# Graph attention inside a four-layer network: scores with keys on partitions, no maximum, and sums over keys on TensorE

## The chip, the cores and the metric

The kernel runs on one core of one Trainium2 chip. The metric is the device time of one execution in microseconds (us). The kernel before takes 2527.05 us, the median of 3 runs (2525.28 to 2527.08). A core has five engines that matter here, each with its own queue: TensorE (PE in the profile, with its weight loads as PEld), VectorE (DVE), ScalarE (ACT), GpSimd (POOL) and SyncE (SP), which issues the transfers.

## The reference

There are 128 graphs of 64 nodes with 256 features in float32, and a 64x64 adjacency for each graph. Four residual layers follow each other: two of attention with 8 heads of 32, one of five gated recurrent steps, and one of gated convolution. Only the two attention layers are touched by the change:

```python
# layer 0                                              # layer 1
scores = einsum('bhqd,bhkd->bhqk', q, k) / sqrt(32)    # the same
scores = where(adj > 0, scores, -9e15)                 # scores + log(adj + 1e-6)
attn = softmax(scores, axis=-1)                        # the same
out = einsum('bhqk,bhkd->bhqd', attn, v)               # the same
x = x + out @ Wo + bo                                  # the same, with Wo.T
```

The `softmax` of the reference subtracts the maximum over the keys, exponentiates, and divides by the sum over the keys. What reads the result next is the normalisation of the following layer.

## The kernel before

The 128 graphs are taken as 64 pairs, two graphs on the 128 partitions, and the pairs in 16 groups of 4. A call of `attend` takes half a group (2 pairs, 256 tokens) through one layer, so there are 16 x 2 x 2 = 64 calls. In each, the 8 heads lie in two banks of PSUM (`i` in 0 and 1 below), so what is done for a bank is done 128 times.

The program records every operation with a cost and its data, and a list scheduler (`plan.run()`) puts them into the queues before anything runs. The attention of one group of graphs, the recurrent steps of the one before it and the convolution of the one before that are interleaved in this way. TensorE's order is fixed when the kernel is built.

The part of `attend` behind the scores, with cuts marked by `...`:

```python
def scores():                           # queries on partitions, keys on the free axis
    for i in range(2):
        for c in range(2):
            for gp in range(2):
                for rh in range(2):
                    ...
                    nc.tensor.matmul(ps[gp * NODES : (gp + 1) * NODES, 2 * c : 2 * c + 2, i, :],
                                     qk[s, c, gp, 0, i * NODES : (i + 1) * NODES],
                                     k_exp[s, c, :, t0 : t0 + NODES], start=True, stop=True)
...
for i in range(2):
    ps, e = pss[i], es[i]
    vec(... scalar_tensor_tensor(e, ps, scale, bias, op0=mult, op1=add))      # L767
    vec(... tensor_reduce(m, e8(), axis=X, op=max))                           # L772
    vec2(... tensor_tensor(e8(), e8(), m to_broadcast, op=subtract))          # L774
    sca(... activation(e, e, AF.Exp))                                         # L776
    vec(... tensor_reduce(z, e8(), axis=X, op=add))                           # L777
    vec(109, ... reciprocal(z, z))                                            # L779
    pool(1000, ... tensor_tensor(e8(), e8(), z to_broadcast, op=mult))        # L780
    pa = bank(f"aT_{name}_{i}")
    def turn(e=e, pa=pa):
        for h in range(4):
            nc.tensor.transpose(pa[:, h * P : (h + 1) * P], e[:, h, :], ident.tile)   # L786
    aT = new("aT", [P, 4, P], 2, f"aT_{name}_{i}")
    pe(437, turn, [e, ident], [pa], holds=[aT], mode=TURN)
    sca(... activation(aT, pa, AF.Copy))                                      # L790
...
def weigh():                            # keys on the contraction axis
    for gp in range(2):
        s = slice(gp * NODES, (gp + 1) * NODES)
        for c in range(2):
            for q in range(4):
                for i in range(2):
                    rows, h = slice(i * NODES, (i + 1) * NODES), 4 * c + q
                    ...
                    nc.tensor.matmul(o[q * HD : (q + 1) * HD, c, s],          # L805
                                     v[rows, gp, h * HD : (h + 1) * HD],
                                     aTs[q // 2][rows, 2 * c + q % 2, s], start=True, stop=True)
def finish():
    for i in range(2):
        vec(... tensor_copy(oT[:, i], po[i][:, :D]))                          # L813
    ...                                 # y = oT times Wo: 4 products          # L818
    vec(... tensor_tensor(xt, py, xt, op=add))                                # L821
```

The weighing of one call waits in a list and is put into TensorE's queue just ahead of the scores of the next call. The bias of the first layer, `neg`, is made once for a group from the adjacency (L1163), and that of the second layer by a logarithm on ScalarE, once for two groups (L336).

Of the kernel before, what the change touches and what calls it, by code (L numbers as in the profile page):

```python
# [54 lines left out]
TURNING = 0.25  # L55
AHEAD = 2.15

FRONT = 0.1  # L60
FRONT_LAST = 0.25
FRONT_SPAN = 0.95
BACK = -0.1
BACK_LAST = 0.35
BACK_SPAN = 0.65
STEP = 0.0
# [3 lines left out]
BACK_END = 0.1  # L70
ENTRY = -0.05
FIRST = -1.2
FIRST_SPAN = 1.2
ORDER = (0, 0, 1, 0, 1, 0)
FUSE = -1.1
FUSE_SPAN = 0.25


# [190 lines left out]


@with_exitstack
def gnn_stack_kernel(ctx: ExitStack, tc: tile.TileContext, a: dict, out: bass.AP):
    nc = tc.nc
    x, adj, nodemask = a["x"], a["adj"], a["nodemask"]
    n_pairs = x.shape[0] // 2
# [94 lines left out]
    with plan.strand(-3.0, 0.1):  # L370


        few = new("few", [P, 7 + PAIRS], 1)

# [4 lines left out]
        fill(slice(1, 1 + PAIRS), 1, -0.5)  # L379
        parity, k_bias = PAIRS + 1, PAIRS + 3  # L380
        fill(slice(parity, parity + 2), 2, 0.0)
        for q in range(4):
            fill(slice(parity + q % 2, parity + q % 2 + 1), 2, 1.0, slice(q * HD, (q + 1) * HD))
        ident = new("ident", [P, P], 1)
        pool(600, lambda: make_identity(nc, ident.tile), [], [ident])
# [13 lines left out]
        def fill_rows():  # L399
            r0 = 0  # L400
            for name in ("L0_gnn_bq", "L0_gnn_bk", "L2_gnn_b_ih", "L2_gnn_b_hh", "L0_gnn_bv"):
                n = a[name].shape[0] // P
                nc.scalar.dma_start(rows.tile[r0 : r0 + n, :], a[name].rearrange("(r p) -> r p", p=P))
                r0 += n
            nc.scalar.dma_start(rows.tile[r0 : r0 + n_pairs, :],
                                nodemask.rearrange("(t a) n -> t (a n)", a=2))
# [6 lines left out]
        def load_first(layer, i):  # L413
            t, j = (first[layer], i) if i < 2 else (first[2], layer)
            dma(256, lambda: nc.sync.dma_start(
                t[:, j], a[f"L{layer}_gnn_W{'qkv'[i]}"].rearrange("(c p) o -> p c o", p=P)), [], [(t, j)])
            return t, j
# [48 lines left out]
    with plan.strand(-0.9, 0.1):  # L466

        w_o, bo = attn[0]
        bvb = new("aT", [P, 4, P], 2, "bvb")
        pbo = bank("bvo")  # L470
        for c in range(2):
            vec(200, lambda c=c: nc.vector.tensor_copy(
                bvb[:, c, :], cols[:, 16 + c : 17 + c].to_broadcast([P, P])), [cols], [(bvb, c)])
            pe(mm(256), lambda c=c, w_o=w_o: nc.tensor.matmul(
                pbo[:, :D], bvb[:, c, :], w_o[:, c, :], start=c == 0, stop=c == 1),
                [(bvb, c), w_o], [pbo])
        vec(dve(256), lambda bo=bo: nc.vector.tensor_tensor(bo.tile, pbo[:, :D], bo.tile, op=ALU.add),
            [pbo, bo], [bo])
# [25 lines left out]
    def power(dst, src, at, eps, n, name):  # L504

        s = new("pw", [P, n], 3, f"pw_{name}")
        vec2(70, lambda: nc.vector.tensor_scalar(s.tile, at(), eps, None, op0=ALU.add), [src], [s])  # L507
        pool(660 if n == 2 else 970, lambda: nc.gpsimd.tensor_tensor(dst.tile, s.tile, few[:, 1 : 1 + n], op=ALU.pow),  # L508
             [s, (few, 1)], [dst], port=2)
# [24 lines left out]

    def norm_relu_t(xt, half, dst, access, writes, name, by_token=None, by_graph=False):

        st = new("st", [P, 2, 6], 3, f"st_{name}")
        mv = new("mv", [P, 2, 2], 3, f"mv_{name}")
        rstd = new("rstd", [P, 2], 3, f"rstd_{name}")
        for i in range(2):  # L540
            p = 2 * half + i
            vec(332, lambda p=p, i=i: nc.vector.bn_stats(st[:, i, :], xt[:, p, :]), [(xt, p)], [(st, i)])
            vec(83, lambda i=i: nc.vector.bn_aggr(mv[:, i, :], st[:, i, :]), [(st, i)], [(mv, i)])
        power(rstd, mv, lambda: mv[:, :, 1], EPS, 2, name)
        xn = new("xn", [P, 2, D], 1, f"xn_{name}")
        for i in range(2):
            p = 2 * half + i
            vec2(325, lambda p=p, i=i: nc.vector.tensor_scalar(
                xn[:, i, :], xt[:, p, :], mv[:, i, 0:1], rstd[:, i : i + 1],
                op0=ALU.subtract, op1=ALU.mult), [(xt, p), mv, rstd], [(xn, i)])  # L550
        if by_token is not None:
# [52 lines left out]
    def attend(layer, xt, half, bias, bias_at, name, plain):  # L604
# [131 lines left out]
        def scores():  # L736
            for i in range(2):
                for c in range(2):
                    for gp in range(2):
                        for rh in range(2):  # L740
                            s = slice(rh * 2 * HD, (rh + 1) * 2 * HD)
                            t0 = (2 * gp + i) * NODES
                            ps = pss[rh].tile.rearrange("p (h i k) -> p h i k", h=4, i=2)
                            nc.tensor.matmul(ps[gp * NODES : (gp + 1) * NODES, 2 * c : 2 * c + 2, i, :],  # L744
                                             qk[s, c, gp, 0, i * NODES : (i + 1) * NODES],
                                             k_exp[s, c, :, t0 : t0 + NODES],
                                             start=True, stop=True)

        es = [new("e", [P, 4, 2 * NODES], 3, f"e_{name}_{i}") for i in range(2)]
        if waiting:  # L750
            _, weigh_last, reads, po_last, oT_last, finish_last = waiting.pop()
            pe(655, weigh_last, reads, po_last, holds=[oT_last], mode=T32)
            pe(860, scores, [qk, k_exp], pss, holds=es, mode=T64)
# [6 lines left out]

        aTs = []
        shape = [P, HEADS, NODES]
        for i in range(2):
            ps, e = pss[i], es[i]
            m = new("smax", [P, HEADS], 3, f"smax_{name}_{i}")
            z = new("ssum", [P, HEADS], 3, f"ssum_{name}_{i}")
# [30 lines left out]
        def weigh():  # L797
# [5 lines that stand above are left out]
# [3 lines left out]
                                             v[rows, gp, h * HD : (h + 1) * HD],  # L806
                                             aTs[q // 2][rows, 2 * c + q % 2, s], start=True, stop=True)

        oT = new("oT", [P, 2, 2, P], 1, f"oT_{name}")

        def finish():
            for i in range(2):
                vec(dve(256), lambda i=i: nc.vector.tensor_copy(  # L813
                    oT[:, i], po[i][:, :D].rearrange("p (c t) -> p c t", c=2)), [po[i]], [(oT, i)])
            py = bank(f"y_{name}")
            for i in range(2):
                for c in range(2):
                    pe(mm(256), lambda i=i, c=c: nc.tensor.matmul(  # L818
                        py[:, i * D : (i + 1) * D], oT[:, i, c, :], w_o[:, c, :],
                        start=c == 0, stop=c == 1), [(oT, i), w_o], [py])  # L820
            vec(dve(512), lambda: nc.vector.tensor_tensor(  # L821
                xt[:, pp : pp + 2, :], py.tile.rearrange("p (t d) -> p t d", t=2), xt[:, pp : pp + 2, :],
                op=ALU.add), [py, (xt, pp), (xt, pp + 1)], [(xt, pp), (xt, pp + 1)])

        waiting.append((xt, weigh, [v, *aTs], po, oT, finish))

    def flush(xt):

        if not waiting or waiting[-1][0] is not xt:
            return  # L830
        _, weigh, reads, po, oT, finish = waiting.pop()
        pe(655, weigh, reads, po, holds=[oT], mode=T32)
        finish()
# [320 lines left out]
    def front(g):  # L1154

        if g % ADJ_GROUPS == 0 and (g // ADJ_GROUPS + 1) * ADJ_GROUPS < n_groups:
# [4 lines left out]
        first = (g % ADJ_GROUPS) * PAIRS  # L1161
        neg = new("neg", [P, PAIRS, NODES], 1, f"neg_{g}")
        vec2(200, lambda: nc.vector.tensor_scalar(  # L1163
            neg.tile, adjq[:, sel, :], 0.0, NEG, op0=ALU.is_le, op1=ALU.mult), [adjq], [neg])
        for layer in range(2):
            if layer and not g % ADJ_GROUPS:
                log_adj(g // ADJ_GROUPS)
            ladj = adj_vals[g // ADJ_GROUPS][1]
            for half in range(2):
                bias = ladj if layer else neg  # L1170
                bias_at = (lambda p, t=ladj, n=first: t.tile.rearrange("p t k -> p (t k)")[:, (n + p) * NODES : (n + p + 2) * NODES]) if layer else (
# [16 lines left out]
        norm = new("norm", [P, PAIRS], 5, f"norm_{g}")  # L1188
        power(norm, deg, lambda: deg.tile, 1e-6, PAIRS, f"deg_{g}")
        adjT = new("adjT", [P, PAIRS, P], 4, f"adjT_{g}")  # L1190
# [14 lines left out]
    def entry(g, xt):  # L1205
# [3 lines left out]
        for half in range(2):  # L1209
            norm_relu_t(xt, half, h, lambda half=half: h[:, :, half * HALF : (half + 1) * HALF],  # L1210
                        [(h, (0, half)), (h, (1, half))], f"{g}_2_{half}", ht)
        return h, ht
# [161 lines left out]
    for at, g, l in events:  # L1374
# [19 lines left out]
        if l + 1 == LAYERS:  # L1394
            with plan.strand(begin[g] + 2 + BACK + (BACK_LAST if g + 2 == n_groups else BACK_END if last else 0), BACK_SPAN):
                back(g, *held.pop(g))
    plan.run()

# [32 lines left out]
```

## Time and profile before

The span is 2523.7 us from the first to the last instruction, at a mean granted TensorE clock of 0.998.

| Part | busy us or length | where it is read |
|---|---|---|
| the products of the recurrent steps (L932), share of the chain | 58% | page, the chain by line (gb 22, gc 17, nb 11, nc 8) |
| transpositions of the weights (aT, L786), share of the chain | 2% | page, the chain by line |
| DVE: L767, L772, L774, L777, L779, 128 each | 82.6, 83.7, 86.1, 84.3, 24.6 us | groups by shape |
| DVE: copy of o (L813), 128 | 50.0 us | groups by shape |
| ACT: Exp (L776) and copy of aT (L790), 128 each | 79.4, 75.2 us | groups by shape |
| POOL: weights times reciprocal (L780), 128 | 149.4 us | groups by shape |
| last TensorE instruction ends | 2516.3 us | timeline |
| last store to DRAM is issued | 2520.5 us | timeline |

How to read it: a busy time is the time in which at least one instruction of the group runs, with its latency. On TensorE the records overlap, and the ends of matmuls are modelled, so for lengths the chain of waits is better: it lists the work that ended last in order of time, each piece from its start to the start of the next. A float32 matmul shows as two MATMUL records, a float32 transposition of 128 columns as one. A group's last column tells how long its engine sat idle just before it, and for whom.

### The profile page before, as it was taken

How to read it: one execution, taken by the hardware profiler on the slowest of the kernel's cores; microseconds unless marked ns; L12 is line 12 of the kernel's file. 1: busy time of each engine (PE TensorE's matmuls, PEld its weight loads, DVE VectorE, ACT ScalarE, POOL GpSimd, SP SyncE). 2: the span in 40 equal slices, each digit the busy share in tenths (PEclk: the TensorE clock that was granted, in tenths of full speed). 3: DMA queues.
4: the chain of work that ended last, by engine and by line, in shares of the span. 5: the costliest groups of instructions: out<-in, count | busy, mean ns of one | idle time of the engine just before them, and what ended most of it. 6: DMA issues, size and time to landing. Idle time of an engine off the chain costs nothing.

```text
span 2523.7 us, 58158 instructions
## 1 busy us (share of the span) xinstructions
PE 2501.1 (99%) x23511; PEld 2150.9 (85%) x23511; DVE 2038.7 (81%) x4632; ACT 1394.8 (55%) x2806; POOL 879.7 (35%) x892
## 2 busy tenths in 40 slices
PE   9999999999999999999999999999999999999998
PEld 7788888888888888888888888888888888888885
DVE  7886787887878888798877978878788887887667
ACT  4456555555556555565555655556555555555444
POOL 5632323424333333333423334243333333333121
PEclk9999999999999999999999999999999999999999
DMA  6511212113121122222113121131211222211120
GB/s 198 174 67 61 93 49 79 62 54 106 51 99 64 61 75 71 79 71 73 59 68 101 50 84 65 52 101 52 98 64 64 68 71 79 71 49 67 49 71 18
DMA packets 78256, 188.47 MB, mean 75 GB/s; under 512 B 14802, under 2 KB 66852, under 8 KB 67108
## 3 DMA queue, kind: packets, MB, share of 16 engines
q1 hardware_dynamic: 77872, 184.71, 21.8%
q8 instruction: 186, 3.05, 0.5%
q14 instruction: 82, 0.67, 0.1%
q10 hardware_dynamic: 116, 0.04, 0.0%
HBM read 166.70 MB, written 18.02 MB: 73 GB/s over the span
## 4 chain that ended last, share of the span: by engine, by line
PE 96%; DVE 3%; ACT 0%; issue 0%; POOL 0%; DMA 0%; DVEq 0%; POOLq 0%; ACTq 0%
PE gb L932 22%; PE gc L932 17%; PE nb L932 11%; PE nc L932 8%; PE qkvb L682 6%; PE qkvc L682 5%; PE y L818 4%; PE agg L972 3%; PE l3b L1254 3%; PE s L744 3%; PE lnT L522 2%; PE l3c L1254 2%; PE aT L786 2%; PE hT L522 2%; PE o L805 2%; PE hom L1321 1%
## 5 line engine op out<-in xcount | busy, mean ns | idle before, releaser
L1041 POOL TENSOR_TENSOR sn<-h,sn 128x512 f32<-128x512 f32 x158 | 209.1, 1327 | 464.1 <-ACT sn L1039 463.7
L508 POOL TENSOR_TENSOR rstd<-pw,few 128x2 f32<-128x2 f32 x128 | 101.6, 794 | 482.9 <-DVE pw L507 459.7
L780 POOL TENSOR_TENSOR e<-e,ssum 128x512 f32<-128x512 f32 x128 | 149.4, 1175 | 315.9 <-DVE ssum L779 284.5
L932 PE MATMUL gb<-Th,w_hh 128*128 128x256 f32 x960 | 248.1, 381 | 0.0
L932 PE MATMUL gb<-Ta,gv 128*128 128x256 f32 x960 | 246.5, 379 | 0.0
L901 POOL TENSOR_TENSOR Th<-h 128x256 f32<-128x256 f32 x160 | 129.5, 829 | 249.6 <-PE nb L932 177.0
L932 PEld LDWEIGHTS gb<-Th,w_hh 128*128 128x128 f32 x960 | 178.1, 190 | 28.6 <-POOL Th L901 0.4
L932 PEld LDWEIGHTS gb<-Ta,gv 128*128 128x128 f32 x960 | 179.6, 190 | 25.3
L1039 ACT ACTIVATE sn<-sn,b_n 128x512 f32<-128x512 f32 x158 | 114.2, 724 | 123.4 <-DVE sn L1037 121.6
L932 PE MATMUL gc<-h,w_hh 128*128 128x256 f32 x640 | 166.1, 382 | 0.1
L932 PE MATMUL gc<-agg,gv 128*128 128x256 f32 x640 | 165.6, 381 | 0.0
L1043 DVE SCALAR_TENSOR_TENSOR sn<-sg,sn 128x512 f32<-128x512 f32 x158 | 107.4, 686 | 58.5 <-POOL sn L1041 58.3
L1024 ACT ACTIVATE sg<-sg,b_rz 128x512 f32<-128x512 f32 x158 | 105.5, 714 | 78.5 <-DVE sg L1004 78.5
L932 PE MATMUL nb<-Th,w_hh 128*128 128x256 f32 x480 | 144.1, 382 | 0.0
L932 PE MATMUL nb<-Ta,gv 128*128 128x256 f32 x480 | 143.0, 380 | 0.0
L901 POOL TENSOR_TENSOR Th<-h,Th 128x256 f32<-128x256 f32 x160 | 139.1, 869 | 10.4 <-DVE h L1045 4.6
L818 PE MATMUL y<-w_L_gnn_Wo,oT 128*128 128x256 f32 x512 | 138.9, 382 | 0.0
L1035 DVE SCALAR_TENSOR_TENSOR sn<-sg,sn 128x512 f32<-128x512 f32 x158 | 110.4, 700 | 34.8 <-ACT sn L1146 31.7
L985 DVE TENSOR_TENSOR Ta<-agg 128x256 f32<-128x256 f32 x160 | 92.3, 588 | 51.5 <-PE nb L932 41.2
L932 PEld LDWEIGHTS gc<-agg,gv 128*128 128x128 f32 x640 | 118.4, 190 | 16.9 <-issue 2.5
L996 ACT ACTIVATE p5g<-gc 128x512 f32<-128x512 f32 x79 | 46.9, 594 | 149.5 <-PE gc L932 149.4
L932 PEld LDWEIGHTS gc<-h,w_hh 128*128 128x128 f32 x640 | 116.3, 190 | 15.5 <-ACT sg L1031 0.5
(224 smaller groups left out, 6943.4 us busy)
## 6 DMA issues: line engine op xcount, KB each, us to landing
gv<-gates SPq DMA_DIRECT2D x80, 1344.0 KB, 6.0
qw<-kept SPq DMA_DIRECT2D x203, 192.0 KB, 2.4
x<-in_x_dram SPq DMA_DIRECT2D x32, 256.0 KB, 5.5
out_dram<-x SPq DMA_DIRECT2D x32, 256.0 KB, 2.3
gates<-gv SPq DMA_DIRECT2D x5, 1344.0 KB, 5.3
adjq<-in_adj_dram SPq DMA_DIRECT2D x8, 256.0 KB, 4.2
gw<-in_L_gnn_weight_dram SPq DMA_DIRECT2D x5, 256.0 KB, 6.4
kept<-s SPq DMA_DIRECT2D x8, 128.0 KB, 3.5
```

Source lines behind the costliest of these rows:

```text
L508: pool(660 if n == 2 else 970, lambda: nc.gpsimd.tensor_tensor(dst.tile, s.tile, few[:, 1 : 1 + n], op=ALU.pow), [s, (few, 1)], [dst], port=2)
L682: nc.tensor.matmul(bk[:, j * P : (j + 1) * P], lhs, rhs, start=first and j == 0, stop=True, skip_group_check=True)
L780: pool(1000, lambda e8=e8, z=z: nc.gpsimd.tensor_tensor(e8(), e8(), z[:, :, None].to_broadcast(shape), op=ALU.mult), [e, z], [e])
L818: pe(mm(256), lambda i=i, c=c: nc.tensor.matmul(py[:, i * D : (i + 1) * D], oT[:, i, c, :], w_o[:, c, :], start=c == 0, stop=c == 1), [(oT ...
L901: pool(690, lambda: nc.gpsimd.tensor_tensor(T[:, i, :], x(), y(), op=ALU.subtract), reads, [(T, i)])
L932: nc.tensor.matmul(bank_[:, col * HALF : (col + 1) * HALF], at(g, n), rhs(), start=first and j == 0, stop=True, skip_group_check=True)
L1024: sca(act(TOK, 1.5), lambda k=k, col=col: nc.scalar.activation(g_v[:, :, k, :], g_v[:, :, k, :], AF.Tanh, bias=b_rz[:, col : col + 1], sca ...
L1035: vec2(dve(TOK), lambda: nc.vector.scalar_tensor_tensor(a_(), r(), 1.0, a_(), op0=ALU.add, op1=ALU.mult), [*ts[0], n_v], [n_v])
L1039: sca(act(TOK, 1.5), lambda: nc.scalar.activation(a_(), a_(), AF.Tanh, bias=b_n[:, oc : oc + 1]), [n_v, b_n], [n_v])
L1041: pool(1230, lambda: nc.gpsimd.tensor_tensor(b_(), hh(), a_(), op=ALU.subtract), [*hp, n_v], [n_v])
L1043: vec2(dve(TOK), lambda: nc.vector.scalar_tensor_tensor(b_(), z(), 1.0, b_(), op0=ALU.add, op1=ALU.mult), [*ts[1], n_v], [n_v])
L1254: pe(mm(384), lambda: nc.tensor.matmul(bk[:, : 3 * P], b(), w3[:, :, n, :], start=first, stop=True, skip_group_check=True), [w3, *reads], ...
```

## The change

Keys take the place of queries on the partitions of the scores, so that the exponentials come out in the layout that the weighing reads. For that the order of query and key weights is exchanged at loading (`order_qkv = "kqv"`). No maximum is subtracted. The adjacency is transposed once per group on TensorE and becomes a factor instead of a bias, 1 or 0 in the first layer and adj + 1e-6 in the second, both times 2^32; the logarithm falls away. The sums over the keys can no longer be taken by VectorE, since keys are on partitions; they come from products with a matrix of ones (each 2^-42) in the midst of the weighing, into the free half of the same PSUM bank. Each sum stands on 32 partitions. One block transposition of 32x32 brings the 8 sums of a partition to the first column of each block, a reciprocal takes 128x8 of them, a second block transposition spreads the results over the 32 partitions again, and one operation multiplies and scales by 2^52. The residual addition takes the scale back (2^-94).

Because the exponential without a maximum can overflow, the means of the third layer's normalisation are kept; if one of them isn't finite, the whole network runs a second time in the old form. That second copy stands in the program behind a branch on a register.

Several constants of the scheduler are set anew as well.

```diff
-AHEAD = 2.15
+AHEAD = 2.0
-FRONT_LAST = 0.25
+FRONT_LAST = 0.15
-BACK_SPAN = 0.65
+BACK_SPAN = 0.7
-ENTRY = -0.05
+ENTRY = 0.05
-FIRST_SPAN = 1.2
+FIRST_SPAN = 1.1
+WEIGH = (655, 950)
 ...
+def gnn_stack_kernel(tc: tile.TileContext, a: dict, out: bass.AP):
+    ...
+        network(tc, a, out, flag)
+        beyond = nc.values_load(flag[0:1, 0:1])
+        with tc.If(beyond > 0, preferred_fallthrough_block=False):
+            network(tc, a, out, None)
 ...
-                            nc.tensor.matmul(ps[gp * NODES : (gp + 1) * NODES, 2 * c : 2 * c + 2, i, :],
+                            i, gp = (inner, outer) if lean else (outer, inner)
+                            to, at = (i, gp) if lean else (gp, i)
+                            nc.tensor.matmul(ps[to * NODES : (to + 1) * NODES, 2 * c : 2 * c + 2, at, :],
 ...
-        es = [new("e", [P, 4, 2 * NODES], 3, f"e_{name}_{i}") for i in range(2)]
+        es = [new("e", [P, 4, 2 * NODES], 4 if lean else 3, f"e_{name}_{i}") for i in range(2)]
 ...
-            pe(655, weigh_last, reads, po_last, holds=[oT_last], mode=T32)
+            pe(WEIGH[lean], weigh_last, reads, po_last, holds=[oT_last], mode=T32)
 ...
-        aTs = []
+        aTs = es if lean else []
 ...
+            if lean:
+                sca(act(512, 0.5), ... activation(e, ps, AF.Exp, scale=scale), [ps], [e])
+                pool(1000, ... tensor_tensor(e, e, mask to_broadcast, op=ALU.mult), [e, bias], [e])
+                continue
 ...
+                if gp or not lean:
+                    continue
+                for q in range(4):
+                    for i in range(2):
+                        rows = slice(i * NODES, (i + 1) * NODES)
+                        nc.tensor.matmul(po[i][q * HD : (q + 1) * HD, D:], ones[rows, :],
+                                         aTs[q // 2].tile.rearrange("p (c r) t -> p r c t", c=2)[rows, q % 2],
+                                         start=True, stop=True)
 ...
+        def divide(i):
+            zt = new("zt", [P, D], 2, f"zt_{name}_{i}")
+            rz = new("rz", [P, HEADS], 2, f"rz_{name}_{i}")
+            vec(dve(256), ... transpose(zt.tile, po[i][:, D:]), [po[i]], [zt])
+            vec(109, ... reciprocal(rz[:, :, None], blocks(zt)[:, :, :1]), [zt], [rz])
+            vec(dve(256), ... transpose(blocks(zt), rz[:, :, None].to_broadcast([P, HEADS, 32])), [rz], [zt])
+            vec(dve(256), ... scalar_tensor_tensor(oT[:, i], zt.tile, WEIGH_UP, po[i][:, :D],
+                op0=ALU.mult, op1=ALU.mult), [po[i], zt], [(oT, i)])
 ...
-            vec(dve(512), ... tensor_tensor(xt, py, xt, op=ALU.add))
+            vec(dve(512), ... scalar_tensor_tensor(xt, py, Y_DOWN if lean else 1.0, xt, op0=ALU.mult, op1=ALU.add))
 ...
+            masks = [new(f"mask{layer}", [P, PAIRS, NODES], 2, f"mask{layer}_{g}") for layer in range(2)]
+            def turn_adj():             # two transpositions of 128x128 for a group
+                ...
+            for layer, (by, op) in enumerate(((0.0, ALU.is_gt), (1e-6, ALU.add))):
+                vec(dve(256), ... tensor_scalar(masks[layer], ps_m, by, MASK_UP, op0=op, op1=ALU.mult))
 ...
+            # once, near the end: means x 0, summed, compared with 0, counted over the partitions
+            # by a product with ones, compared with 128 into `flag`
```

## The prediction, made before the changed kernel was run

> **What bounds the kernel now.** I read the page first, then the chain of waits, then the groups by shape, then the list of who waited for whom, and last the order of the instructions in the two programs. The page gives the span, the busy time of each engine, and the chain that ended last.
>
> ```profile
> span 2523.7 us, 58158 instructions
> PE 2501.1 (99%) x23511; PEld 2150.9 (85%) x23511; DVE 2038.7 (81%) x4632; ACT 1394.8 (55%) x2806; POOL 879.7 (35%) x892
> PE 96%; DVE 3%; ACT 0%; issue 0%; POOL 0%; DMA 0%; DVEq 0%; POOLq 0%; ACTq 0%
> ```
>
> The reader is to see one engine, PE, at 99%, and the chain running on it for 96% of the span. A busy PE need not be a full PE, because matmuls overlap, so I looked at the chain piece by piece, which gives start to start times. This is a stretch from the middle; its columns are the start in us, the length in us, the line and the number of records.
>
> ```profile
> 1074.21 1.03 PE s L744 x32
> 1075.25 0.93 PE agg L972 x64
> 1076.18 1.06 PE gb L932 x4
> 1077.24 0.67 PE qkvb L682 x6
> 1077.90 0.67 PE qkvc L682 x6
> 1078.58 0.87 PE gc L932 x4
> ```
>
> There is no hole between the pieces: each starts where the one before it ends, and four 256-column records always take 0.86 us, except just behind small-tile work, where they take 1.06. The last view is PE's own list of waits, of which the three longest entries are
>
> ```profile
> PE gb L932 <- ACT agg L978: 2.4, 3, 1.2
> PE lnT L522 <- DVE xn L548: 1.8, 3, 0.9
> PE aT L786 <- POOL e L780: 1.7, 1, 1.7
> ```
>
> The whole list sums to about 15 us in 2523.7. So the time is the sum of what stands in PE's queue, plus some 22 us (2523.7 minus 2501.1) of ramp at the two ends. Work taken off DVE, ACT or POOL is worth only what it removes of those 22 us; work taken off PE is worth its full length.
>
> **What the Trainium skill says.** "TensorEngine Tiling (Array Packing)", Tiling Modes: a 64x32 mode has 8 independent tiles, and a change of mode drains the engine. The trace agrees: the 0.2 us by which the gb piece above is longer behind agg is that drain. "TensorE: Matmul & The Clock Gate", Measured speedup vs the span model: 9 packed tiles gave 6.32 times, not 9. Here 8 tiles in the weighing give less than 8 too (worked out below). "VectorE: DVE Perf Modes", The three transpose paths: the DVE transposition is of 32x32 blocks only and takes 311 ns for 128x128 bf16; no run here shows one yet. "Runtime: NRT & Kernel Launch", Instruction fetch mechanics: a taken branch to a target outside the fetched window waits for a fetch. The kernel before has no such branch at its end, so its trace cannot say.
>
> **The change part by part, on PE.** These are the groups by shape that matter; the columns are count, busy time, mean of one record in ns, and the idle time before it.
>
> ```profile
> L786 PE MATMUL aT<-ident,e 128*128 128x128 f32 x512 | 76.9, 273 | 1.8 <-POOL e L780 1.7
> L744 PE MATMUL s<-kexp,qk 64*64 64x128 f32 x2048 | 71.0, 275 | 0.0
> L805 PE MATMUL o<-aT,v 64*32 64x64 f32 x4096 | 55.3, 224 | 0.0
> ```
>
> Busy time in this view counts each record's latency, so I take lengths from the chain instead.
>
> Removed: the transpositions of the weights aT. 512 records are 128 groups of 4 (64 halves of attention, two banks each). In the chain a group is always 0.44 us: 128 x 0.44 = 56 us off PE.
>
> Moved, no change: the score products are the same 2048 records with query and key exchanged; the number of blocks of small-tile work in the queue is 140 before and 139 after, so the drains stay the same.
>
> Added: the sums over keys, 8 products of 256 columns with ones in each weighing, in the same 64x32 mode, so no new drain. Each matmul here is two records (the 2048 products of the weighing show as 4096), so 16 records of 256 columns. A 256-column record takes 0.216 us (0.86 / 4). If all 8 tiles run at once, that is 2 x 0.216 = 0.43 us for one weighing. Check with the weighing as it is: 64 records of 64 columns, a quarter of 0.216 or 0.054 us each, are 3.46 us one after another; the chain shows 0.79 us for the piece, of which about 0.15 is the drain, so 3.46 / 0.64 = 5.4 tiles at a time on average. At 5.4 the ones cost 16 x 0.216 / 5.4 = 0.64 us; but the short records are held up by their issue and weight loads, and long ones hide those. The scheduler's own table in the change raises a weighing from 655 to 950 ns, or 0.30. I choose 0.38: 64 x 0.38 = 24 us, from 19 (at 0.30) to 41 (at 0.64).
>
> Added too: 2 transpositions of the adjacency for each of 16 groups of graphs, 32 records of 0.44 / 4 = 0.11 us: 3.5 us. Sum for PE: -56 + 24 + 3.5 = -28.5 us.
>
> **The other engines.** For one of 128 banks DVE loses the biased copy (about 677 ns in its groups), the maximum (671), the subtraction (688), the sum (672), the reciprocal (192) and the copy of o (414): 3314 ns. It gains two block transpositions, which I estimate at the 414 ns of the 128x256 copy from PSUM, a reciprocal of 192, and a scale-and-multiply of about 470 as the other 128x256 operation with two inputs from PSUM (L1324, 473): 1490 ns. The saving is 128 x 1.82 = 233 us; the two masks of a group give back 32 x 0.41 minus 16 x 0.29, or 8. DVE falls from 2039 to some 1815 us.
>
> ACT loses the copies of aT (75.2 us), the logarithms (5.8), and nearly all table loads: the program after has one where the one before has 17 (17 x 1.28 = 22 us, 16 of them off). It falls to about 1293. POOL's multiplication by the reciprocal becomes one by the mask, same shape and count, about 149 us. All this is beside PE. I credit it with 4 us of the ramp: in the windows of the first 120 us DVE is busy for 98 (38 of the 40 between 40 and 80) and PE idle for 7.5, and half of that may go.
>
> **The tail.** The result of the range test is loaded into a register on each engine, and each branches past a second copy of the network that is not run. The tests and the one-column product run earlier, beside other work. Loads and branches on PE, ACT and POOL lie beside DVE's last operations (PE is done 7 us before the end), but on DVE and SP they come last. I put them at 4 us, an estimate from nothing better than the 2.3 us that a store to DRAM takes to land here. The schedule's constants were changed too; I count 0 for them.
>
> Sum: 2527 - 28.5 - 4 + 4 = 2498.5, say 2498 us, 1.1% below.
>
> **The rivals.** First, that the time follows DVE: 233 us less of 2039 would then make a large gain, below 2450. Against it is the chain, with DVE at 3%, and the windows, where PE is busy for 1800 of the 1800 us between 400 and 2200. Second, that DVE's new chain behind the weighing becomes the wait: transposition, reciprocal, transposition, multiplication for two banks in a row, some 3 us by the durations above, where two copies took 0.83. The output products y then start 2 us later. For it: PE's queue is fixed by the schedule, so a late oT stops PE; if a third of the 64 halves lost 1.5 us each, that would be 32 us, the whole gain. Against it: DVE is freer, and the schedule was made anew. In the order of instructions, what stands on PE between the end of a weighing and the first y comes to 1.9 us in the median before, and to 3.2 after, with 1.9 as the least, by the lengths above; the first bank's four operations take 1.5. Third, that the sums pack badly: 0.64 us or more, leaving 2515; if four tiles at a time were the limit, 16 x 0.216 / 4 = 0.86 us, 55 us in all, and the gain is gone. Against that, the weighing now runs faster than four at a time would allow (3.46 / 4 = 0.86 against 0.64). Fourth, that the range test comes out true and the network runs again: the time would double. I give that 1%.
>
> **The range and the chances.** From 0.30 us for the sums with a tail of 2 us, 5 us less of ramp and a few us from the schedule's constants, I get 2484; from 0.64 us with a tail of 6, some 2514. To be faster by over 2% it would have to go below 2476.5, 22 us beyond my figure, which needs the sums to be nearly free: 0.06. Slower than 2577 needs the doubled run or the second rival at its worst: 0.02. Within 2%: 0.92.
>
> **What would show it right or wrong.** PE still at 98 to 99% and the chain still on it; a weighing piece in the chain of about 0.79 + 0.38 = 1.17 us; no piece for aT; DVE near 1815 us and ACT near 1290; block transpositions near 414 ns; the last store followed by some 4 us more than before. I am wrong if PE's list of waits has y waiting for oT for more than 15 us in total, if the weighing takes over 1.5 us, or if the span ends far behind the last store.

## The result and the profile after

The changed kernel takes 2507.45 us (median of 4, 2507.14 to 2508.67) against 2526.16 for the kernel before in the same series: a ratio of 0.9929, with a 95% interval of 0.9915 to 0.9943. That is 18.7 us less, where 2498 us, 28 less, was predicted, in a range of 2484 to 2514.

The same three lines of the page, now for the changed kernel:

```profile
span 2505.0 us, 58714 instructions
PE 2483.1 (99%) x24057; PEld 2131.6 (85%) x24057; DVE 1875.7 (75%) x4396; ACT 1304.8 (52%) x2654; POOL 889.4 (36%) x894
PE 97%; DVE 2%; ACT 0%; issue 0%; POOL 0%; DMA 0%; DVEq 0%; ACTq 0%; POOLq 0%
```

PE is still at 99% and the chain still runs on it. DVE has lost 163 us and ACT 90, and the span only 18.7. A weighing and a group of transpositions in the chain of waits of the kernel before (start, length, line, records):

```profile
1012.26 0.79 PE o L805 x53
1028.54 0.44 PE aT L786 x4
```

And a piece of the chain of the changed kernel with a weighing in it:

```profile
1077.32 0.38 PE o L843 x32
1077.71 0.46 PE o L851 x10
1078.16 0.45 PE o L843 x28
1078.61 1.03 PE s L775 x32
```

The weighing (the three `o` pieces) now runs from 1077.32 to 1078.61, 1.29 us, where the one before took 0.79. These are also the medians of all 64 weighings. The added 0.50 us came with the products with ones (L851). Behind the scores the weights' transpositions (aT) are gone. The groups by shape show what stands on the engines (count, busy us, mean ns, idle before):

```profile
L851 PE MATMUL o<-e,ones 64*32 64x256 f32 x1024 | 49.8, 385 | 0.0
L861 DVE STREAM_TRANSPOSE zt<-o 128x256 f32<-128x256 f32 x128 | 52.2, 429 | 48.7 <-PE o L843 47.8
L863 DVE STREAM_TRANSPOSE zt<-rz 128x256 f32<-128x256 f32 x128 | 50.0, 416 | 0.0
```

No row has aT. A block transposition takes 429 or 416 ns, close to the 414 that were estimated. The end of the program is in the timeline. The last store is issued here, first in the kernel before and then in the changed one:

```profile
2520.53 0.37 SPq L1346 DMA_DIRECT2D out_dram<-x  x1
```

```profile
2497.65 0.37 SPq L1431 DMA_DIRECT2D out_dram<-x  x1
```

From there to the end of the span it is 2523.7 - 2520.5 = 3.1 us before and 2505.02 - 2497.65 = 7.4 us after. So the work itself got 22.9 us shorter, and the tail took 4.2 us back. At the other end, the windows of the first 120 us (length, then busy time of PE, PEld, DVE, ACT, POOL) are, before and after:

```profile
0.00:120.00 120.00, 112.47 (x1164) 88.73 (x1165) 98.12 (x246) 58.06 (x109) 68.17 (x85) 1.00 0.56 185
```

```profile
0.00:120.00 120.00, 116.54 (x1245) 93.21 (x1246) 80.80 (x232) 45.80 (x92) 73.68 (x90) 1.00 0.58 197
```

PE is idle there for 7.5 us before and 3.5 after. The sum of what these views show is -56 (128 groups of four transpositions, 0.44 each) + 32 (64 x 0.50) + 3.5 (masks) + 4.2 (tail) - 4 (first 120 us) = -20.3, against 18.7 of the spans. The other 1.6 us are a balance of small items. From each TensorE record's start to the next one's, less its streaming time (0.216 us for 256 columns), the holes under 0.15 us add up to 5 or 6 us more than before; longer waits outside the first 120 us, and the products with the adjacency, of which more now stand next to other small-tile work, give 2 to 3 us each back.

### The profile page after: what moved, and what is told of

Same layout as the page of the kernel before. It is cut to its first block, busy times and chain, and to the rows that moved or that the text cites. A ratio compares the mean times of both kernels' runs of the same rounds, so it can differ in the third digit from the quotient of the medians.

```text
span 2505.0 us, 58714 instructions
## 1 busy us (share of the span) xinstructions
PE 2483.1 (99%) x24057; PEld 2131.6 (85%) x24057; DVE 1875.7 (75%) x4396; ACT 1304.8 (52%) x2654; POOL 889.4 (36%) x894
## 4 chain that ended last, share of the span: by engine, by line
PE 97%; DVE 2%; ACT 0%; issue 0%; POOL 0%; DMA 0%; DVEq 0%; ACTq 0%; POOLq 0%
PE gb L994 22%; PE gc L994 17%; PE nb L994 11%; PE nc L994 8%; PE qkvb L711 6%; PE qkvc L711 5%; PE y L879 4%; PE agg L1034 3%; PE l3b L1339 3%; PE s L775 2%; PE l3c L1339 2%; PE lnT L547 2%; PE hT L547 2%; PE o L843 2%; PE o L851 1%; PE gv L930 1%
## 5 line engine op out<-in xcount | busy, mean ns | idle before, releaser
L963 POOL TENSOR_TENSOR Th<-h 128x256 f32<-128x256 f32 x160 | 120.4, 772 | 333.6 <-PE nb L994 230.6
L533 POOL TENSOR_TENSOR rstd<-pw,few 128x2 f32<-128x2 f32 x128 | 94.9, 741 | 382.6 <-DVE pw L532 380.6
L799 POOL TENSOR_TENSOR e<-e,mask 128x512 f32<-128x512 f32 x128 | 176.2, 1396 | 105.9 <-ACT e L797 105.9
L1105 DVE SCALAR_TENSOR_TENSOR sn<-sg,sn 128x512 f32<-128x512 f32 x158 | 107.4, 686 | 62.9 <-POOL sn L1103 62.6
L963 POOL TENSOR_TENSOR Th<-h,Th 128x256 f32<-128x256 f32 x160 | 144.8, 905 | 8.6 <-DVE h L1107 2.9
L1097 DVE SCALAR_TENSOR_TENSOR sn<-sg,sn 128x512 f32<-128x512 f32 x158 | 118.6, 758 | 37.1 <-ACT sn L1208 30.5
L1107 DVE SCALAR_TENSOR_TENSOR h<-sn 128x512 f32<-128x512 f32 x158 | 122.2, 780 | 5.6 <-ACT e L797 0.5
```

The lines of the kernel that those rows point to most:

```text
L799: pool(1000, lambda e=e: nc.gpsimd.tensor_tensor(e.tile, e.tile, bias_at(pp)[:, None, :].to_broadcast([P, 4, 2 * NODES]), op=ALU.mult), [e ...
L963: pool(690, lambda: nc.gpsimd.tensor_tensor(T[:, i, :], x(), y(), op=ALU.subtract), reads, [(T, i)])
L1097: vec2(dve(TOK), lambda: nc.vector.scalar_tensor_tensor(a_(), r(), 1.0, a_(), op0=ALU.add, op1=ALU.mult), [*ts[0], n_v], [n_v])
L1105: vec2(dve(TOK), lambda: nc.vector.scalar_tensor_tensor(b_(), z(), 1.0, b_(), op0=ALU.add, op1=ALU.mult), [*ts[1], n_v], [n_v])
L1107: vec2(dve(TOK), lambda: nc.vector.scalar_tensor_tensor(hh(), b_(), 0.5, a_(), op0=ALU.mult, op1=ALU.add), [n_v], hp)
```

## The experiments

The theory: the time is what stands in TensorE's queue, and the terms above make up the change. The rivals: the gain comes from VectorE's relief; the new operations on VectorE hold TensorE up; or the order of the instructions, which the scheduler makes anew for every change, counts for as much as the operations.

### The removal alone

```diff
-            pa = bank(f"aT_{name}_{i}")
-            def turn(e=e, pa=pa): ...           # 4 transpositions
-            pe(437, turn, [e, ident], [pa], holds=[aT], mode=TURN)
-            sca(... activation(aT, pa, AF.Copy))
-            aTs.append(aT)
+            aTs.append(e)                       # 4 buffers for e instead of 3
```

> The kernel before with the transpositions of the weights and their copy by ScalarE left out; the weighing reads the weights untransposed, so the output is not the reference's. If the time is the sum of TensorE's queue, all of 128 x 0.44 = 56 us goes: about 2470 us. If the waits of other engines fill the place (the rival that the gain was hidden), clearly less goes: 2485 us or more.

Measured: 2487.2 us, a ratio of 0.9852 (0.9835 to 0.9868), so some 37 us less and not 56. A third of what left the queue did not arrive. The windows of the steady part show a first piece of it (PE, PEld, DVE, ACT, POOL as above), the kernel before first:

```profile
400.00:2200.00 1800.00, 1800.00 (x17279) 1564.96 (x17271) 1486.85 (x3438) 1018.09 (x2077) 633.53 (x622) 1.00 0.22 72
```

```profile
400.00:2200.00 1800.00, 1795.37 (x17103) 1546.62 (x17102) 1532.25 (x3485) 988.27 (x2013) 628.37 (x632) 1.00 0.22 73
```

PE has 4.6 us of holes where it had none, and DVE is denser, 1532 us against 1487. A busy time hides holes that the latency of a record covers. In the times from one TensorE record's start to the next one's, less the streaming, the records of full-array work outside the first 120 us have 9 us more in holes over 0.15 us (20.6 against 11.7) and 5 us more in shorter ones; the weighings are 3 us longer in total and the first 120 us 2 us. These 19 us are about what is missing. The theory in its plain form falls: what is taken off TensorE's queue is not all gained.

### VectorE's relief alone, and with the removal

```diff
-            vec(dve(512), ... tensor_reduce(m.tile, e8(), axis=AX.X, op=ALU.max), [e], [m])
-            vec2(dve(512), ... tensor_tensor(e8(), e8(), m to_broadcast, op=ALU.subtract), [e, m], [e])
```

In the kernel before:

> The kernel before without the maximum and its subtraction: 128 x (0.671 + 0.688) = 174 us less on VectorE, nothing less on TensorE. If the queue of TensorE is the bound: 2520 to 2527 us (at most some of the 7 us of ramp). If VectorE had a share in the bound: below 2510 us.

Measured: 2528.44 us, a ratio of 1.0009 (1.0002 to 1.0016). So 256 operations less on VectorE bring nothing, in fact 2 us more. The order of the instructions is another here too, but the holes over 0.15 us stay as they were (12.3 us against 11.7), so no gain shows there either. The same edit on top of the first one:

> The kernel before without the transpositions of the weights and without the maximum and its subtraction (the output is not the reference's). Without the transpositions alone it took 2487 us, 17 us more than 2526 - 56 = 2470, and its list of waits on TensorE had grown. If what is missing is waits on the busy VectorE (83% there), taking 174 us off it brings the time to 2470 to 2477 us. If it is the new order of instructions, it stays at 2484 us or more.

Measured: 2477.29 us, a ratio of 0.9797 (0.9781 to 0.9813); the removal alone had 0.9852. Here the same relief is worth 0.55% or 14 us by the ratios, and 10 us by the times themselves (2487.2 and 2477.3, each from a series with its own kernel before). The same window:

```profile
400.00:2200.00 1800.00, 1796.76 (x17187) 1549.84 (x17186) 1406.43 (x3304) 992.33 (x2010) 629.93 (x628) 1.00 0.22 73
```

VectorE is back from 1532 to 1406 us in that window, and the holes fall from 4.6 to 3.2; in the first 120 us PE's idle time falls from 7.6 to 3.1. The holes over 0.15 us fall from 20.6 to 15.6. So the two belong together: with TensorE's queue shorter by 56 us, the other engines have less time for the same work, and VectorE's relief takes away a part of the waits that came up. How much of the 10 to 14 us is another order of instructions, these two runs don't separate.

### The products with ones, doubled

```diff
-                for q in range(4):
-                    for i in range(2): ...      # the 8 products with ones
+                for _ in range(2):
+                    for q in range(4):
+                        for i in range(2): ...
```

> The changed kernel with the products with ones issued twice (the second overwrites the first with the same values). By TensorE's sum each of 64 weighings grows by at least 2 x 0.216 = 0.43 us, by 0.50 if they always cost what they added: 28 to 32 us more, 2535 to 2540 us. If they are partly hidden, less: 2515 to 2530 us.

Measured: 2537.64 us, a ratio of 1.0049 (1.0032 to 1.0066), 30 us above the changed kernel. One weighing in the chain:

```profile
1027.71 0.38 PE o L843 x32
1028.09 0.89 PE o L852 x26
1028.98 0.45 PE o L843 x28
1029.43 1.06 PE gc L995 x4
```

It runs from 1027.71 to 1029.43, 1.72 us. The second set costs 1.72 - 1.29 = 0.43 us, which is two rounds of 0.216 us with all eight tiles at work, and nothing of it is hidden (64 x 0.43 = 27.5 of the 30 us). The first set costs 0.50, 0.07 more; where these stand, the next run asks.

### Their place in the weighing

```diff
-                if gp or not lean:
+                if not gp or not lean:
                     continue
```

> The changed kernel with the products with ones behind all products of the weighing instead of between its halves; the scheduler sees no difference, so all else stands where it stood. The weighing is now 1.29 us for 0.79 + 0.43 by streaming, so 0.07 us are lost at the seams. If the seam in the middle costs: a weighing of 1.22 us and 4 us less, 2503 us. If long records behind short ones cost as much: 2507 us; more if the middle place hides weight loads.

Measured: 2508.58 us, a ratio of 0.9930 (0.9913 to 0.9946), no difference. One weighing:

```profile
1076.96 0.72 PE o L843 x49
1077.68 0.03 PE o L851 x2
1077.71 0.03 PE o L843 x2
1077.75 0.50 PE o L851 x14
```

From 1076.96 to 1078.25 it is 1.29 us again. The place "amid the weighing" is worth nothing in time, and the 0.07 us are not the price of a seam in its middle: they stay when that seam is gone. What they are is not shown.

### The products with ones in bfloat16

First with a copy of the weights, since their sums need little precision:

```diff
+                e16 = new("e16", [P, 4, 2 * NODES], 3, ..., bfloat16)
+                sca(act(512), ... activation(e16.tile, e.tile, AF.Copy), [e], [e16])
-                        nc.tensor.matmul(po[i][...], ones[rows, :], aTs[q // 2]...)
+                        nc.tensor.matmul(po[i][...], ones16[rows, :], e16s[q // 2]...)
-            zt = new("zt", [P, D], 2, ...)
+            zt = new("zt", [P, D], 1, ...)
-WEIGH = (655, 950)
+WEIGH = (655, 800)
```

The masks are in bfloat16 as well.

> The changed kernel with the products with ones on a bfloat16 copy of the weights (made by ScalarE; the masks are bfloat16 as well, to make room), everything else in float32. A bfloat16 product should be one record where the float32 one is two, so 8 of 256 columns in place of 16. By TensorE's sum at least one of the two rounds of 0.216 us goes: 64 x 0.22 = 14 us or more, 2494 us or less; if the single records are also shorter, 2486 us. If the added 77 us on ScalarE make new waits: 2500 us or more.

Measured: 2516.95 us, a ratio of 0.9958 (0.9944 to 0.9972): 7 (by the ratios) to 9.5 us slower than the changed kernel, though each weighing is shorter:

```profile
1084.31 0.39 PE o L847 x32
1084.69 0.16 PE o L855 x5
1084.86 0.34 PE o L847 x22
1085.20 1.03 PE s L775 x32
```

This is 0.89 us instead of 1.29, so 64 x 0.40 = 25 us left the queue, and some 35 us came in. PE's list of waits has a new head:

```profile
PE adjT L1284 <- ACT hT L552: 7.5, 11, 0.7
PE l3b L1343 <- DVE mask L1240: 3.4, 11, 0.3
```

Neither wait stands in the changed kernel's list, but they are only 11 of the 35 us. From start to start, the holes over 0.15 us went from 8.9 to 30.6 us. And TensorE's queue has 173 blocks of small-tile work in place of 139. In the medians such a block costs 0.33 us at its edges (0.09 us ahead of it, 0.14 behind its last record, 0.10 in the record after), so the 34 more are some 11 us, and their number is a matter of order alone. The waits may come from the added copies on ScalarE, from the order that they and the new table entry brought about, or from the single buffer for `zt`. To see what the shorter products are worth without all this, the next version has no copy, two buffers and float32 masks, and the order stays as it was: it reads the upper halves of the float32 weights through a strided view.

```diff
-                        nc.tensor.matmul(po[i][...], ones[rows, :], aTs[q // 2]...[rows, q % 2], ...)
+                        nc.tensor.matmul(po[i][...], ones16[rows, :], aTs[q // 2]...[rows, q % 2]
+                                         .bitcast(mybir.dt.bfloat16)[:, :, 1::2], ...)
-WEIGH_UP = 2.0 ** 52
+WEIGH_UP = 2.0 ** 52 * 0.9973
```

> The changed kernel with the products with ones reading the upper 16 bits of the float32 weights as bfloat16 (a strided view, no copy; the mean truncation is taken back by a factor 0.9973 in the scale). Costs in the scheduler's table are left as they are, so every instruction stands where it stood. If TensorE's queue sum is the bound, the weighing falls from 1.29 to about 0.89 us as with the bfloat16 copy, and 64 x 0.40 = 25 us go: 2480 to 2485 us. If the copy's run lost its gain for another reason than its order of instructions (a bound elsewhere): 2495 us or more.

Measured: 2486.41 us, a ratio of 0.9847 (0.9830 to 0.9863), 21 us below the changed kernel. The weighing has the same pieces, 0.90 us in the median of all:

```profile
1067.88 0.39 PE o L843 x32
1068.26 0.17 PE o L851 x4
1068.43 0.35 PE o L843 x25
```

With the order held, 21 of the 25 us arrive; the other 4 are in new holes. So TensorE's sum is the bound, and the copy's run did not lose its gain to a bound elsewhere. Some 11 us of it went to the order; for the waits, the share of the copies, of the order and of the buffer stays open.

### The test at the end

```diff
         network(tc, a, out, flag)
-        beyond = nc.values_load(flag[0:1, 0:1])
-        with tc.If(beyond > 0, preferred_fallthrough_block=False):
-            network(tc, a, out, None)
```

> The changed kernel without the register load, the branch and the second copy of the network behind it (the test for overflow is still computed, but nothing reads it). From the last store to the end the trace has 7.4 us with it and 3.1 us in the kernel before. If the branch is the cause: about 4.2 us less, 2503 us, and 3.1 us behind the last store. If the tail has another cause: 2507 us.

Measured: 2502.83 us, a ratio of 0.9911 (0.9894 to 0.9927). This is 4.6 us below the changed kernel; the two intervals overlap, so the trace has to decide. The last store is issued at

```profile
2497.14 0.37 SPq L1428 DMA_DIRECT2D out_dram<-x  x1
```

of a span of 2500.3: 3.1 us behind it, as in the kernel before. The register load and the branch cost 4.2 us. The load itself is short. These are the records of SP in the changed kernel behind its last store (duration in ns: minimum, median and maximum; first and last start in us):

```profile
L283 SPq TENSOR_LOAD <-flag x1: 484/484/484, 2498.1 to 2498.1; - x1
L284 SPq COMPARE_BRANCH  x2: 38/46/53, 2498.6 to 2501.1; - x2
L284 SPq EVENT_SEMAPHORE  x8: 17/17/17, 2500.5 to 2501.0; - x8
L1530 SPq EVENT_SEMAPHORE  x10: 17/28/28, 2503.7 to 2505.0; - x10
```

Behind each of the two branches SP has nothing: 1.8 us from the first (2498.6) to the semaphores at 2500.5, and 2.6 us from the second (2501.1) to 2503.7. The store, issued at 2497.65, lands beside the first of them, if it takes the 2.9 us of the median store. The DMA queues of this stretch (2497.7 to the end) have, besides the store,

```profile
q14 instruction: 6, 0.05, 2.1%
q8 instruction: 1, 0.02, 1.0%
```

and none of these two queues in the version without the branch (2493 to the end). So instructions are fetched at this place because of the branch. That a branch waits for such a fetch is what the Trainium skill says of one that is taken to a place outside the fetched window ("Runtime: NRT & Kernel Launch", Instruction fetch mechanics). The two gaps fit it; that these very fetches end them is not shown.

### The wide reciprocal

```diff
-            vec(dve(256), ... transpose(zt.tile, po[i][:, D:]))
-            vec(109, ... reciprocal(rz[:, :, None], blocks(zt)[:, :, :1]))
-            vec(dve(256), ... transpose(blocks(zt), rz[:, :, None].to_broadcast([P, HEADS, 32])))
+            vec(dve(256), ... reciprocal(zt.tile, po[i][:, D:]))
```

> The changed kernel with one reciprocal of 128x256 straight from the sums in place of the two block transpositions and the reciprocal of 128x8. If TensorE's queue is the bound: 2505 to 2510 us, whatever VectorE then needs. If the chain of four operations ahead of the output products held TensorE up: below 2503 us if the wide reciprocal is short (about 0.4 us), above 2512 us if it takes over 1 us.

Measured: 2658.78 us, a ratio of 1.0519 (1.0501 to 1.0536). The instructions that touch `zt`, first here and then in the changed kernel:

```profile
L859 DVE RECIPROCAL zt<-o x128: 1694/1750/1759, 26.4 to 2398.9; 128x256 f32<-128x256 f32 x128
```

```profile
L861 DVE STREAM_TRANSPOSE zt<-o x128: 394/434/452, 26.6 to 2252.9; 128x256 f32<-128x256 f32 x128
L862 DVE RECIPROCAL rz<-zt x128: 152/169/206, 27.4 to 2254.0; 128x8 f32<-128x8 f32 x128
L863 DVE STREAM_TRANSPOSE zt<-rz x128: 394/408/453, 27.6 to 2254.5; 128x256 f32<-128x256 f32 x128
```

The reciprocal of 256 takes 1750 ns; the three that it replaces take 434 + 169 + 408 = 1011. VectorE is at 75% of the span as in the changed kernel, so it isn't full, and still the time is 151 us above that kernel's. PE's list of waits tells how:

```profile
PE y L874 <- DVE oT L860: 57.4, 32, 2.4
PE lnT L547 <- DVE xn L577: 13.8, 28, 1.2
```

The table told the scheduler 335 ns for this reciprocal (`dve(256)` in the code is 256 x 1.042 + 68), where it had 335 + 109 + 335 = 779 for the three. So y stands too early in TensorE's fixed order, and what stands behind it waits too: from start to start, TensorE's holes over 0.15 us grow from 8.9 to 129.5 us. The granted clock (0.990 against 0.999) is no rival: a record of 256 columns is still 0.216 us. What was expected under "whatever VectorE then needs" was wrong, and the other expectation, over 2512 us if the reciprocal takes over 1 us, came true. The second rival of the prediction is a real mechanism; the changed kernel escapes it. Its list of waits has no entry for y, since the first y stands 3.3 us behind the weighing in the median (2.0 in the kernel before) and the eight operations of both banks took 2.3 us in one weighing of the timeline (1078.63 to 1080.94).

### The scheduler's constants

```diff
-AHEAD = 2.0          # and FRONT_LAST, BACK_SPAN, ENTRY, FIRST_SPAN
+AHEAD = 2.15         # the values of the kernel before
```

> The changed kernel with the scheduler's constants of the kernel before (AHEAD 2.15, FRONT_LAST 0.25, BACK_SPAN 0.65, ENTRY -0.05, FIRST_SPAN 1.2). If the operations make the gain and the constants nothing: 2505 to 2511 us. If the new constants brought a good part of the 19 us: 2515 us or more.

Measured: 2514.52 us, a ratio of 0.9948 (0.9931 to 0.9965), against 0.9929 for the changed kernel: 5 to 7 us slower, though the intervals overlap. The other way round, the new constants in the kernel before:

> The kernel before with the scheduler's constants of the change. The old constants made the changed kernel 7 us slower. If the new ones are better in themselves: about 2519 us. If constants only suit the program they were chosen for: 2526 to 2540 us.

Measured: 2557.12 us, a ratio of 1.0126 (1.0109 to 1.0143), 30 us slower, and 17 us above the most that was expected. The operations are the same as before, only their order differs. PE's list of waits begins with

```profile
PE l3b L1254 <- ACT lu L1262: 7.0, 11, 0.6
PE l3b L1254 <- ACT hT L527: 3.4, 12, 0.7
```

These come 11 and 12 times, with 16 groups of graphs: the order is repeated, and one bad place in it is paid again and again. They are 10 of the 30 us. From start to start, holes over 0.15 us grew by 17 us (11.7 to 28.5) and shorter ones by 7; TensorE's queue also has 165 blocks of small-tile work in place of 140. The constants were chosen for the program that they stand in. A part of the 19 us, up to 7, may be this choice.

### A version that beats both

The upper halves and no branch together, with 745 ns for the weighing in the table:

> The same without the register load, the branch and the second copy, and with 745 ns for the weighing in the scheduler's table (1.29 - 0.40 - 0.15 of drain). By the sum 2507 - 25 - 4.6 = 2478 us; but the table makes a new order of instructions, which by the runs so far can be worth 5 to 30 us either way: 2470 to 2505 us.

Measured: 2481.51 us, a ratio of 0.9823 (0.9806 to 0.9839), 26 us below the changed kernel. It leaves out the repetition for scores that overflow, and its sums come from truncated weights.

## Why the prediction was right, and where its steps were off

The time lies in the range, and the bound is as read: TensorE's queue. By the steps:

- **The transpositions, -56 us.** Their records are gone, and the length of 0.44 us was right. The step "work taken off PE is worth its full length" failed: alone the removal gave 37 us, and 19 came back as waits, holes and longer weighings. Its other half, "work taken off DVE, ACT or POOL is worth only what it removes of those 22 us", failed in this form too. It held for the relief alone (ratio 1.0009), but together with the removal the same relief was worth 10 to 14 us. In the change both come together, with 233 us forecast off VectorE, so the sum was nearly kept. The prediction did not foresee this, and that the two errors met is luck.
- **The products with ones, 24 us.** This is the term that was mis-sized most: 0.50 us for a weighing and not 0.38, so 32 us. The estimate for eight tiles at once, 0.43, was right to the second digit for a second set (the first costs 0.07 more); I discounted it because of the table's 0.30, which no trace had shown. That is 8 of the 9.5 us by which the time was missed.
- **The masks, 3.5 us, and the first 120 us, 4 us.** Both as predicted (32 records; 7.5 to 3.5 us of idle time).
- **The tail, 4 us.** 4.2 measured. The estimate rested on the time that a store takes to land, and the trace shows gaps behind branches: luck.
- **The constants, 0 us.** Not settled to the microsecond, but not nothing: 5 to 7 us here, and 30 in the other program.
- **VectorE at 1815 us, ACT at 1290.** ACT came to 1305. VectorE came to 1876: removing 256 operations of 671 and 688 ns took only 105 us off its busy time in the run without the maximum, not 174. Of the 69 us, 39 are records of other operations that became longer, and 30 are overlap that went with the removed ones (two transpositions in a row took 0.78 us in the timeline, not 0.86). So a mean duration times a count says too much. POOL's multiplications came to 176 us where 149 were expected.
- **The rivals.** That the time follows VectorE is refuted by the relief alone. The wait of y for oT does not occur in the changed kernel, but did with the longer chain. The packing of the sums was a little worse than chosen, far from four at a time. The network did not run twice.
- **The range.** Its upper end, 2514, does not follow from its own terms: 0.64 us for the sums and 6 for the tail give 2527 - 56 + 41 + 3.5 - 4 + 6 = 2517.5.

## What to carry to other kernels

Where an engine is full and its order fixed, count its queue from start-to-start times, and don't discount a streaming time without a trace that shows less. What is removed from that queue arrives only if the other engines can still deliver in the shorter time, so removals on the full engine and relief of the next busy one should be made and measured together. With a scheduler, also run one version in which every instruction keeps its place: a change in order alone cost more than the operations gained here (30 us against 19).

## What was not expected of the hardware

- A reciprocal on VectorE costs about (1750 - 169) / (256 - 8) = 6.4 ns for each element of a partition, where a copy of 256 takes 414 ns in all (the 256 are read from PSUM, the 8 from SBUF). Two block transpositions to reduce it to 8 elements pay.
- A weighing of 64x32 tiles took 1.29 us with the long products in its middle and at its end.
- A bfloat16 product of 256 columns reads every second 16-bit element of a float32 tile as fast as a packed bfloat16 tile (the pieces of the eight of them are 0.17 and 0.16 us).
- The multiplication on GpSimd by the mask took 1396 ns in the mean, where that by the reciprocal took 1175, and 1208 with masks in bfloat16. Nothing waited for it, and the cause was not looked for.
